# Adjacency masks of the first attention layer: comparing a quarter of the row pairs in SBUF ahead of the transpose, and copying their masks out of PSUM with ScalarE

## The chip, the cores and the metric

The kernel runs on one core of a Trainium2 chip. The metric is the device time of the whole program in microseconds (us). It was run three times; the number that counts is the median. One more execution was taken with the hardware profiler, and all views of the profile come from that one.

The engines are called by the profile's short names: PE is TensorE's matrix multiplication, PEld its weight load, DVE is VectorE, ACT is ScalarE, POOL is GpSimd, SP is SyncE, which here only issues DMAs.

## The reference

The program is two layers over a graph of 4096 nodes with 256 features each. A layer is graph attention and then a feed-forward part. What matters here is the attention of the first layer: four heads, each with 64 outputs, and an adjacency matrix of 4096 x 4096 int32 zeros and ones that masks the scores.

```python
h = jnp.einsum('nd,mdo->mno', x, W)
f_src = jnp.einsum('mno,mo->mn', h, a1)
f_dst = jnp.einsum('mno,mo->mn', h, a2)
e = jax.nn.leaky_relu(f_src[:, :, None] + f_dst[:, None, :], LEAK)
e = jnp.where(adj[None, :, :] > 0, e, NEG_INF)
attn = jax.nn.softmax(e, axis=-1)
out = jax.nn.elu(jnp.einsum('mnk,mko->mno', attn, h))
return jnp.transpose(out, (1, 0, 2)).reshape(x.shape[0], -1)
```

Node n sums over its neighbours k. On the chip k must lie on the partitions, so the kernel needs the adjacency turned: `adj[n, k]` as a mask with k on the partitions and n along the row.

## The kernel before

The function `attention` (called in line 686 for the first layer) walks over the 4096 nodes n in five column chunks of 4, 7, 7, 7 and 7 tiles of 128 nodes. For each chunk it goes over the four heads, and within a head over 16 pairs q of neighbour tiles (a tile is 128 neighbours k, so there are 32 tiles, numbered j). One chunk, head and pair is a **unit**: 64 units make a chunk, 16 a head. In a unit of a 7-tile chunk

- ScalarE makes `st`, two steps (`step_of`, line 483) of 128x896, one for each tile of the pair: whether the score is on the positive or the negative branch of the leaky relu;
- VectorE combines `st` with the mask of the pair into `m1` (line 617, 128x1792), and for two thirds of the pairs subtracts to get `m2` (line 632);
- TensorE multiplies the masks with the values (`products`, line 569), adding up in `acc`, for the unit before the present one (`LAG` is 1).

ScalarE runs two units ahead (`LEAD`, line 550). `st` and `m1` have three buffers, `m2` two. When a head is finished, ScalarE copies parts of `acc` into `lo` (line 492), VectorE adds them up into `u` (line 496), and `close` finishes the rows in small pieces during the first units of the next head; one of them is an `Exp` on ScalarE (line 521).

The masks are made only in this layer. For a pair of tiles j and j + 1, `load_rows` (line 205) lets GpSimd issue a DMA that reads 256 columns of the adjacency for the nodes of a chunk, casts them to bf16, and leaves them in `rows` (buffers of the pool `stream`, four of them). `turn` (line 214) transposes one tile's columns on TensorE into the PSUM tile `tp_m` (line 219; bf16, one buffer). `to_mask` (line 224) has VectorE compare out of PSUM into SBUF: the result is 1 or 0, or, for the pairs that `turned(q)` names (every third), 0 or -1; hence its two branches, lines 227 and 229.

This is done at two places:

- For chunk 0, `first_masks` runs in the preparation, beside the projections of the features (the first 103 us or so). The masks stay in SBUF in `m`.
- For the chunk after the present one, `make` (line 528) is a generator that the main loop takes one step further at the end of each unit (line 646). A tile is turned in one unit and compared in the next, so that nearly all of a chunk's 64 units do one half of a tile. The result goes into `ms` (two buffers of a pair each), which SP's queue writes to `edges` in DRAM (line 542); `load_mask` reads it back for the next chunk.

In the main loop VectorE and ScalarE keep the order in which the program is written, because of

```python
with tc.manual_schedule(engines={mybir.EngineType.DVE, mybir.EngineType.Activation}):
```

Everything that `make` emits in a unit is therefore placed after that unit's `step_of`, `m1`, `m2` and a piece of `close`. In the preparation the order on the engines is the framework's.

Of the kernel before, what the change touches and what calls it, by code (L numbers as in the profile page):

```python
# [16 lines left out]
OP = mybir.AluOpType  # L17
# [27 lines left out]
def gnn_ffn_kernel(ctx: ExitStack, tc: tile.TileContext, a: dict, out: bass.AP):  # L45
    nc = tc.nc
    x, adj = a["x"], a["adj"]
    N = x.shape[0]
    NT = N // P
# [75 lines left out]
    def turned(q):  # L125
        return q % 3 == 0
# [45 lines left out]
    def attention(tag, src, norm, w, others, chunks, first, ends, following):  # L172
# [7 lines left out]
        with ExitStack() as scope:  # L180
# [9 lines left out]
            masks, arow, f1b = {}, {}, {}  # L190
# [14 lines left out]
            def load_rows(c, j):  # L205
                nt = chunks[c]
                arow[c, j] = rows_in().bitcast(BF16).rearrange("p (t n) -> p t n", n=2 * P)

                nc.gpsimd.dma_start(  # L209
                    arow[c, j][:, :nt, :],  # L210
                    adj[starts[c] * P : (starts[c] + nt) * P, j * P : (j + 2) * P].rearrange("(t p) n -> p t n", p=P),
                )

            def turn(pool, c, j):

                nt = chunks[c]
                tp = pool.tile([P, 8 * P], BF16, name="tp_m")
                for t in range(nt):
                    nc.tensor.transpose(  # L219
                        tp[:, t * P : (t + 1) * P], arow[c, j - j % 2][:, t, (j % 2) * P : (j % 2 + 1) * P], ident16  # L220
                    )
                return tp

            def to_mask(dst, tp, c, j):
                w = chunks[c] * P
                if turned(j // 2):
                    nc.vector.tensor_scalar(dst[:, :w], tp[:, :w], 0.0, -1.0, op0=OP.is_le, op1=OP.add)
                else:
                    nc.vector.tensor_scalar(dst[:, :w], tp[:, :w], 0.0, None, op0=OP.is_gt)  # L229

            def first_masks(pool, j):

                g = j // 8
                if j % 8 == 0:
                    masks[0, g] = mask.tile([P, 8, CM * P], BF16, name="m")
                for jj in (j, j + 1):
                    to_mask(masks[0, g][:, jj % 8, :], turn(pool, 0, jj), 0, jj)
                if j % 8 == 6:
                    w = chunks[0] * P
                    nc.sync.dma_start(  # L240
                        edges[g * 8 : (g + 1) * 8, :, :w].rearrange("j p n -> p j n"), masks[0, g][:, :, :w]
                    )

            with ExitStack() as ps:
# [163 lines left out]
                if not first:  # L408
                    load_mask(0, 0)
                made_masks = 0  # L410
                late = [functools.partial(make, prep, small_ps, get(prep)) for get, make in others]
                for g in range(NG + 2):
                    if g + 2 < NG:
                        load(g + 2)
                    if 2 <= g < NG:
                        columns(g)
                    if 1 <= g <= NG:
                        now = products(g - 1)
                    if 2 <= g:
                        lower(g - 2)  # L420
                    if g < 2:
                        columns(g)
                    if g == 0 and late:
                        late.pop(0)()
                    if 1 <= g <= NG:
                        upper(g - 1, *now)
                    if first:
                        for _ in range(2 if g in (1, 2, 3, 4, 5, 6) else 1):
                            if made_masks < NT:
                                first_masks(ps_m, made_masks)  # L430
                                if made_masks + 6 < NT:
                                    load_rows(0, made_masks + 6)
                                made_masks += 2
                    elif g in (2, 4, 6):
                        load_mask(0, g // 2)
                    if g in (3, 5) and late:
                        late.pop(0)()
# [90 lines left out]
            def make(c):  # L528

                n0, w = starts[c] * P, chunks[c] * P  # L530
                load_rows(c, 0)
                load_rows(c, 2)
                for j in range(NT):
                    if j % 2 == 0:
                        st = made.tile([P, 2, CM * P], BF16, name="ms")
                        if j + 4 < NT:
                            load_rows(c, j + 4)
                    tp = turn(ps_m, c, j)
                    yield
                    to_mask(st[:, j % 2, :], tp, c, j)  # L540
                    if j % 2 == 1:
                        nc.sync.dma_start(
                            edges[j - 1 : j + 1, :, n0 : n0 + w].rearrange("j p n -> p j n"), st[:, :, :w]
                        )
                    if j < NT - 4:
                        yield

# [39 lines left out]
            with tc.manual_schedule(engines={mybir.EngineType.DVE, mybir.EngineType.Activation}):  # L587
# [3 lines left out]
                for at in range(len(units) + LAG):  # L591
# [5 lines left out]
                    if at < len(units):  # L597
                        c, h, q = units[at]
                        w = chunks[c] * P
                        if q == 0 and h == 0 and first and c + 1 < len(chunks):  # L600
                            making = make(c + 1)
                        if q == 4 and at + NJ < len(units):
                            load_f1(*units[at + NJ - 4][:2])
# [46 lines left out]
            c, h, q = units[-1]  # L650
# [31 lines left out]
    for n in range(2):  # L682
        av = a[f"L1_gnn_a{n + 1}"]
        for got, to in zip(weights(f"g{n + 1}", a[f"L1_gnn_W{n + 1}"], av[:, :D], av[:, D:], not n), (gw, makers)):
            to.append(got)
    attention("g0", x, True, w0, [make, *makers], [4, 7, 7, 7, 7], True, to_rows(x1d, x), [x1d])


# [272 lines left out]
    for n in range(2):  # L961
        attention(
            f"g{n + 1}",
            h1d if n else x2d,
            not n,
            gw[n],
            [],
            [8, 8, 8, 8],
            False,
            to_rows(x3d, x2d) if n else to_rows(h1d),  # L970
            [x3d, runs_of] if n else [h1d],
        )
# [7 lines left out]
    with ExitStack() as scope:  # L980
# [16 lines left out]
        with ExitStack() as rs:  # L997
# [16 lines left out]
            for g in range(NG + 2):  # L1014
# [12 lines left out]
                if 1 <= g <= NG:  # L1027
                    u = g - 1
                    t = rows.pop(u)
# [83 lines left out]
            for i in range(2):  # L1113
# [33 lines left out]
                op0=OP.mult,  # L1147
                op1=OP.is_lt,
# [206 lines left out]
        for g in range(NG + 3):  # L1355
            if g < NG:
                ys[g] = [back(g, i) for i in range(2)]
            if 3 <= g:
                for i, y in enumerate(ys.pop(g - 3)):
                    for r in range(G):  # L1360
                        t = (g - 3) * G + r
# [34 lines left out]
```

## Time and profile before

| | |
|---|---|
| median of three runs | 3407.78 us (3407.05 to 3408.95) |
| the profiled execution: time, span | 3416.7 us, 3415.0 us |
| busy share of the span | PE 92%, PEld 81%, DVE 91%, ACT 81%, POOL 37% |
| preparation of the first layer, masks of chunk 0 | about 0 to 103 us |
| chunk 0 (4 tiles), masks of chunk 1 made | about 103 to 203 us |
| chunks 1, 2, 3 (7 tiles), masks of the next chunk made | about 203 to 653 us |
| chunk 4 (7 tiles), no masks made | about 653 to 793 us |
| L227 and L229 in chunks 1 to 4 (`ms`) | 48 and 80 instructions of 618 ns |
| L227 and L229 in chunk 0 (`m`) | 12 and 20 instructions of 421 and 417 ns |
| L219, the transposes into `tp_m` | 1024 of 128x128 |

A row of the profile names line, engine, operation, the tile that is written and those that are read, and the shape. "Idle before" is the time in which the engine stood still just ahead of such instructions, and the arrow names what ended most of it. The recorded duration of an instruction can overlap with the next one's on the same engine, so the time by which an instruction holds its queue is read from the starts of two that follow each other.

### The profile page before, as it was taken

Reading aid. Unit: us, or ns where it says so; the run is one execution under the profiler, and the core shown is the slowest. Engines: PE = TensorE matmul, PEld = TensorE weight load, DVE = VectorE, ACT = ScalarE, POOL = GpSimd, SP = SyncE. Lnnn points to the kernel's source line nnn. Section 1 sums busy time; section 2 is a strip of 40 time slices with the busy share of each in tenths; the row PEclk is TensorE's granted clock in tenths of the full one; section 3 lists DMA queues with packets and bytes.
Section 4 is the critical chain, followed back from the end, with each engine's and each line's share of the span. In section 5 each row is a group of like instructions: output and inputs, shape, how many; then the busy total and the mean of one; then the engine's idle time right before and its main releaser. Section 6 shows DMA issues by size and latency. Waiting matters only on the chain.

```text
span 3415.0 us, 84150 instructions
## 1 busy us (share of the span) xinstructions
PE 3149.6 (92%) x34367; PEld 2767.7 (81%) x34367; DVE 3105.9 (91%) x5992; ACT 2754.6 (81%) x3422; POOL 1248.2 (37%) x1166
## 2 busy tenths in 40 slices
PE   7889999997999999999988999999889999985995
PEld 4788888885888888888866999999779999984884
DVE  7999999998999999999978999999899999996445
ACT  3888888897888888888857999999799999982221
POOL 3210010005999999999982000000300000002662
PEclk9999999998999999999999999999999999996997
DMA  7997886603334343334363032230503131314224
GB/s 147 174 230 145 192 184 142 193 23 86 69 68 69 69 68 67 69 69 69 67 162 119 27 119 73 75 119 24 172 20 125 33 131 50 113 48 144 89 90 186
DMA packets 533659, 351.63 MB, mean 103 GB/s; under 512 B 350589, under 2 KB 483866, under 8 KB 533274
## 3 DMA queue, kind: packets, MB, share of 16 engines
q1 hardware_dynamic: 452210, 287.12, 30.8%
q0 software_dynamic: 73920, 52.97, 9.9%
q10 hardware_dynamic: 7144, 6.16, 0.6%
q8 instruction: 271, 4.44, 0.5%
q14 instruction: 114, 0.93, 0.1%
HBM read 248.01 MB, written 68.81 MB: 93 GB/s over the span
## 4 chain that ended last, share of the span: by engine, by line
DVE 32%; POOL 31%; issue 15%; PE 14%; ACT 6%; DMA 2%; ACTq 0%; DVEq 0%; POOLq 0%; SPq 0%
DVE m L617 17%; POOL th L869 16%; PE acc L569 10%; POOL z_rs L892 7%; ACT st L483 4%; POOL z_rs L893 3%; DVE rows L632 3%; DVE m L632 2%; POOL yd L1316 2%; POOL gx L1250 2%; DVE u L496 1%; DVE v L382 1%; DVE ms L229 1%; PE ph L308 1%; DVE u L506 1%
## 5 line engine op out<-in xcount | busy, mean ns | idle before, releaser
L569 PE MATMUL acc<-vals,m 128*128 128x130 f16 (+1 forms) x19456 | 1722.1, 233 | 72.3 <-DVE m L632 42.8
L483 ACT ACTIVATE st<-f1b,f2b 128x1024 bf16<-128x1024 f32 (+2 forms) x1664 | 1659.1, 1073 | 98.9 <-DVE m L617 92.4
L569 PEld LDWEIGHTS <-m 128*128 128x128 bf16 x19456 | 1516.9, 98 | 170.6 <-DVE m L632 65.0
L617 DVE TENSOR_TENSOR m<-st,m 128x2048 bf16<-128x2048 bf16 (+2 forms) x832 | 929.1, 1134 | 15.2 <-ACT st L483 14.9
L569 PE MATMUL acc<-vals,rows 128*128 128x130 f16 x5120 | 614.1, 221 | 15.1 <-DVE rows L632 15.1
L905 PE MATMUL po<-wT,zT 128*128 128x256 f32 x1920 | 575.6, 382 | 7.0 <-ACT zT L888 7.0
L908 PE MATMUL po<-w,zT 128*128 128x256 f16 x3840 | 577.4, 273 | 1.9 <-DMA zT<-z 1.9
L869 POOL TENSOR_TENSOR th<-th,y 128x1024 f32<-128x1024 f32 x240 | 569.2, 2372 | 25.4 <-ACT th L868 5.6
L908 PEld LDWEIGHTS <-zT 128*128 128x128 f16 x3840 | 376.1, 98 | 163.0 <-DMA zT<-z 2.9
L569 PEld LDWEIGHTS <-rows 128*128 128x128 bf16 x5120 | 490.0, 96 | 20.5 <-DVE rows L632 20.1
L632 DVE TENSOR_TENSOR rows<-m,m 128x2048 bf16<-128x2048 bf16 x320 | 391.7, 1224 | 10.2
L845 DVE SCALAR_TENSOR_TENSOR y<-po,z_rs,bias 128x256 f32<-128x256 f32 x928 | 384.4, 477 | 1.9 <-PE tp L838 0.7
L881 DVE BATCH_NORM_STATS2 z_st<-z 128x6 f32<-128x256 f32 x960 | 335.8, 413 | 0.0
L905 PEld LDWEIGHTS po<-wT,zT 128*128 128x128 f32 x1920 | 290.7, 191 | 16.9 <-ACT zT L888 8.6
L106 POOL TENSOR_TENSOR ln_rstd<-ln_rstd,mhalf 128x4 f32<-128x4 f32 x24 | 34.1, 1421 | 645.4 <-DVE ln_rstd L105 630.5
L857 ACT ACTIVATE z<-th 128x1024 f32<-128x1024 f32 x240 | 251.2, 1047 | 8.6 <-POOL th L869 8.3
L209 POOL DMA_DIRECT2D rows<-in_adj_dram x80 | 72.8, 910 | 492.9 <-PE tp_m L219 479.8
L868 ACT ACTIVATE th<-y 128x1024 f32<-128x1024 f32 x240 | 249.8, 1041 | 0.0
L892 POOL TENSOR_TENSOR z_rs<-z_rs,mhalf 128x4 f32<-128x4 f32 x240 | 245.8, 1024 | 0.0
L888 ACT COPY zT<-tp 128x512 f32<-128x512 f32 x240 | 140.4, 585 | 109.0 <-PE tp L838 108.9
L632 DVE TENSOR_TENSOR m<-m,m 128x1792 bf16<-128x1792 bf16 (+1 forms) x200 | 202.2, 1011 | 13.1 <-PE acc L569 0.5
L462 POOL MEMSET hs<- 128x4 f32 x3 | 0.3, 101 | 582.3 <-DVE u L513 582.3
(251 smaller groups left out, 3165.1 us busy)
## 6 DMA issues: line engine op xcount, KB each, us to landing
m<-edges SPq DMA_DIRECT2D x32, 2048.0 KB
rows<-in_adj_dram POOLq DMA_DIRECT2D x64, 448.0 KB
edges<-ms SPq DMA_DIRECT2D x64, 448.0 KB
m<-edges SPq DMA_DIRECT2D x16, 1792.0 KB
f1b<-fd SPq DMA_DIRECT2D x32, 512.0 KB
rows<-x1d SPq DMA_DIRECT2D x16, 512.0 KB
y<-yd SPq DMA_DIRECT2D x16, 512.0 KB
f1b<-fd SPq DMA_DIRECT2D x16, 448.0 KB
```

The lines of the kernel that those rows point to most:

```text
L483: nc.scalar.activation(steps[at][:, s, :w], f1b[c, h][:, :w], AF.Relu, bias=f2b[:, 2 * q + s, h : h + 1], scale=BIG)
L569: nc.tensor.matmul(acc[:, i, cols], lhs[:, s, rows], v[:, cols], start=(j == 0 and n_ == 0), stop=(j == NT - 1 and n_ == 1), skip_group_ch ...
L617: nc.vector.tensor_tensor(m1[:, :, :w], st[:, :, :w], m, OP.logical_and if turned(q) else OP.min)
L632: nc.vector.tensor_tensor(m2[:, :, :w], m, m1[:, :, :w], OP.subtract)
L845: nc.vector.scalar_tensor_tensor(y[:, g * G + r, :], po[:, r, :], rstd[:, r : r + 1], last if end else bias, op0=OP.mult, op1=OP.add,)
L857: nc.scalar.activation(z, th.pop(u), AF.Silu, scale=0.01)
L868: nc.scalar.activation(th[at], y[:, g * G : (g + 1) * G, :], AF.Tanh, scale=0.01)
L869: ins = nc.gpsimd.tensor_tensor(th[at], th[at], y[:, g * G : (g + 1) * G, :], OP.add)
L881: nc.vector.bn_stats(st[:, r, :], z[:, r, :])
L892: nc.gpsimd.tensor_tensor(rs[u], rs[u], mhalf, OP.pow)
L905: nc.tensor.matmul(po[:, r, :], src[:, r * P : (r + 1) * P], wT, start=True, stop=False)
L908: nc.tensor.matmul(po[:, r, :], src16[:, part * G + r, :], w16[:, other, :], start=False, stop=(part == 1 and other == 1),)
```

## The change

The function `compared` picks the tile pairs 1, 5, 9 and 13 of the 16: a quarter. For these pairs `compare` runs on VectorE over the loaded rows in SBUF, in place, both tiles of the pair and all tiles of the chunk in one instruction (128x1792 bf16, in chunk 0 128x1024), before TensorE turns them. The comparison is the same as that of `to_mask`, with 1 and 0 or 0 and -1. TensorE then transposes finished masks, and `to_mask` has ScalarE copy them from PSUM, two copies for a pair (128x896, in chunk 0 128x512). The other twelve pairs of a chunk are left as they were.

In `make` the comparison for the pair that begins at j + 1 is placed just after the second tile of the pair before has been turned into a mask and its write to `edges` was issued; in `first_masks` it stands ahead of the pair's transposes. The loads of the rows, the number of transposes, the buffers and the writes to `edges` stay.

```diff
+            def compared(j):
+
+                return j // 2 % 4 == 1
+
+            def compare(c, j):
+
+                t = arow[c, j][:, : chunks[c], :]
+                if turned(j // 2):
+                    nc.vector.tensor_scalar(t, t, 0.0, -1.0, op0=OP.is_le, op1=OP.add)
+                else:
+                    nc.vector.tensor_scalar(t, t, 0.0, None, op0=OP.is_gt)
+
             def to_mask(dst, tp, c, j):
                 w = chunks[c] * P
-                if turned(j // 2):
+                if compared(j):
+                    nc.scalar.copy(dst[:, :w], tp[:, :w])
+                elif turned(j // 2):
                     nc.vector.tensor_scalar(dst[:, :w], tp[:, :w], 0.0, -1.0, op0=OP.is_le, op1=OP.add)
                 else:
                     nc.vector.tensor_scalar(dst[:, :w], tp[:, :w], 0.0, None, op0=OP.is_gt)
...
                 g = j // 8
+                if compared(j):
+                    compare(0, j)
                 if j % 8 == 0:
...
                             edges[j - 1 : j + 1, :, n0 : n0 + w].rearrange("j p n -> p j n"), st[:, :, :w]
                         )
+                        if j + 1 < NT and compared(j + 1):
+                            compare(c, j + 1)
                     if j < NT - 4:
                         yield
```

## The prediction

> **What bounds the kernel now.** The change touches only the first attention layer, so I read the engines' busy time by stretch first. The three stretches below lie in column chunks 1, 2 and 3, each of which also makes the masks of the chunk after it. Columns: stretch, its length, then busy us and instruction counts of PE, PEld, DVE, ACT, POOL, the TensorE clock, the DMA share, GB/s.
>
> ```profile
> 205.00:350.00 145.00, 134.62 (x1927) 124.53 (x1927) 137.22 (x169) 124.53 (x137) 14.88 (x16) 0.99 0.80 180
> 355.00:500.00 145.00, 135.20 (x1946) 124.68 (x1945) 138.49 (x169) 124.21 (x136) 14.87 (x16) 1.00 0.76 168
> 505.00:650.00 145.00, 134.85 (x1942) 124.37 (x1940) 138.14 (x168) 123.86 (x136) 11.16 (x12) 1.00 0.74 170
> ```
>
> VectorE is busy 95%, TensorE 93%, ScalarE 86%. No engine has much room, so shares don't decide. The waits do (who waited, for whom: total, times, longest; 105 to 650 us):
>
> ```profile
> ACT st L483 <- DVE m L617: 72.4, 113, 2.4
> PEld L569 <- DVE m L632: 52.0, 96, 1.4
> PE acc L569 <- DVE m L632: 34.6, 90, 1.3
> DVE u L496 <- ACT lo L492: 13.9, 27, 1.0
> ```
>
> ScalarE and TensorE both wait for VectorE's masked pairs; VectorE waits for them only at the change of head (`u` after `lo`). The chain of waits over 0 to 700 us tells where in a head (start, length, piece):
>
> ```profile
> 420.49 1.73 PE acc L569 x27
> 422.61 3.96 PE acc L569 x56
> 426.96 3.00 PE acc L569 x44
> 432.42 1.08 DVE m L632
> ...
> 457.90 1.73 PE acc L569 x27
> ```
>
> The same pieces come back after 457.90 − 420.49 = 37.4 us: one head (16 units), 2.34 us a unit. For 9.5 us before a head ends the chain is TensorE's; from 432 to 458 it is VectorE's. So VectorE work in those 26 us lengthens the head, as long as TensorE can follow. That is where the changed pair falls.
>
> **What the mask work costs.** From the instructions on tile `tp_m`:
>
> ```profile
> L229 DVE TENSOR_SCALAR ms<-tp_m x80: 615/618/620, 112.4 to 643.4; 128x896 bf16<-128x896 bf16 x80
> L229 DVE TENSOR_SCALAR m<-tp_m x20: 402/417/426, 30.0 to 99.8; 128x512 bf16<-128x512 bf16 x20
> ```
>
> Recorded 0.618 us, but the queue is held less. The timeline has one comparison and its successor:
>
> ```profile
> 448.04 0.62 DVE L227 TENSOR_SCALAR ms<-tp_m 128x896 bf16<-128x896 bf16 x1
> 448.31 5.69 ACT L483 ACTIVATE st<-f1b,f2b 128x896 bf16<-128x896 f32 x6
> 448.57 1.08 DVE L617 TENSOR_TENSOR m<-st,m 128x1792 bf16<-128x1792 bf16 x1
> ...
> 455.70 1.79 PE L569 MATMUL acc<-vals,m 128*128 128x130 f16 x28 [0.33 <-DVE m L632]
> ...
> 457.90 1.73 PE L569 MATMUL acc<-vals,m 128*128 128x130 f16 x27 [0.41 <-DVE m L632]
> ```
>
> 448.57 − 448.04 = 0.53 us per comparison: successive VectorE instructions overlap by about 0.08. The six ScalarE steps take 5.69 / 6 = 0.95 each. The bracketed waits are TensorE's room, used below.
>
> **What the Trainium skill says.** Page "VectorE: DVE Perf Modes", section "The perf-mode tier table": `tensor_scalar` on bf16 runs at four elements a cycle from SBUF, at most two from PSUM. The trace agrees on the second (896 elements at two a cycle of 0.96 GHz are 467 ns, plus some 150, against 618); it has no bf16 SBUF `tensor_scalar`, so the four are not shown. Page "SBUF — State Buffer", section "SBUF: two separate sides": a VectorE op in a two-port mode and a GpSimd op exclude each other for a whole instruction, descriptor writing for GpSimd's DMAs included. No run here shows that; its cover is below.
>
> **The change, part by part.** In chunks 1 to 4 a head of 16 units turns 8 mask rows, four pairs; one pair changes, always the head's second. 4 × 4 = 16 pairs, plus 4 in chunk 0.
>
> *Removed:* two PSUM comparisons per pair on VectorE, 2 × 0.535 = 1.07 us (chunk 0: 2 × 0.34 = 0.68, from 0.418 less the 0.08).
>
> *Added on VectorE:* one in-place comparison of 128x1792. The page's walk-through ("Side-by-side", about 158 cycles fixed) gives, as an estimate, (1792/4 + 158) / 0.96 = 0.63 us, held 0.55. Bounds: 0.47 if only the elements counted; 1.00 at two a cycle, as the 128x1792 `tensor_tensor` row L617 holds the queue; 1.9 at one. I take 0.55. Chunk 0, 128x1024: 0.43, held 0.35. **VectorE saves 1.07 − 0.55 = 0.52 per pair, 0.33 in chunk 0.** All: 16 × 0.52 + 4 × 0.33 = 9.6 us.
>
> *Added on ScalarE:* two copies per pair. No 128x896 PSUM copy exists, but two sizes of `scalar.copy` out of PSUM do:
>
> ```profile
> L328 ACT COPY hc<-ph 128x512 f32<-128x512 f32 x48 | 26.4, 582 | 20.6 <-DVE fs L322 18.9 <-DVE fs L326 1.6
> L279 ACT COPY xT<-tp 128x1024 f32<-128x1024 f32 x16 | 16.2, 1012 | 26.3 <-PE tp L114 26.2
> ```
>
> 582 + (384/512) × 430 = 905 ns, held 0.82 (lower if bf16 out were cheaper, upper 0.95 as the steps of L483): 1.64 us per pair. Its cover is ScalarE's idle time, 145 − 124.2 = 20.8 us in 3.9 heads, **5.4 per head**.
>
> *Where they stand in the queues.* Counting units from the head's start, `compare` follows the comparison in unit 3, the copies end units 5 and 7.
> - VectorE: 0.55 later from unit 3, level after unit 5, 0.52 ahead after unit 7. TensorE's turn of that pair comes in unit 4, after `products(3)`, at 440.07 in this head; the comparison would end near 439.3, so TensorE doesn't wait for it.
> - ScalarE: the first copy follows the step for unit 7, which ends near 441.8; the turn it reads ends at 440.6. No wait. The next step started at 442.69 (after a wait for VectorE): the 0.82 fits. The second copy follows the step for unit 9 and the head's `Exp`, near 448.3. It pushes the six steps at 448.31 back by 0.82, to end at 454.8. The step for unit 12 is then done near 454.8 and is used at 458.3; the waits at 454.55, 456.68 and 459.41 swallow the delay.
> - TensorE: the turn at 449.95 needs `tp_m` back (one buffer); the second copy ends at 449.2. It then catches up by its waits of 0.28, 0.33 and 0.41 after 450: 1.0 against 0.52 needed. So nearly all of the 0.52 gets through; I count 0.50.
> - DMA queues: each row load is awaited by a turn about 30 us after it is issued (20 in chunk 0's stage), and a 448 KB load takes a few us, so VectorE's new wait for it ends at once. GpSimd's load issues (0.93 us) run right after the second turn of a pair, over a us before `compare`; they waited 447 us anyhow. SP's write of the pair waits for the second copy rather than for VectorE, about 0.6 us later; nothing but loads for the next head is behind it.
>
> *Sum.* Chunks 1 to 3: 12 heads × 0.50 = 6.0. Chunk 0's stage (103 to 203 us, 24.9 us a head, the 16 DMA engines busy all through): the ScalarE waits that follow the copies, 0.47 and 0.59 in the head at 128 us, are less than twice 0.82, so ScalarE hands on only some 0.3 of the 0.52: 4 × 0.3 = 1.2. Masks of chunk 0 in the preparation: VectorE is busy 78 of 105 us there, with much waiting for others, so 0.8 of 1.3. **Together 8.0 us** of the profiled execution's 3416.7 (span 3415.0). That execution was 8.9 above the median 3407.78; the stage is 1/6 of it, so I take 8.0 off the median: **3399.8 us**. What is late next is TensorE: after the 0.5 its room at the end of a head is 0.5 more.
>
> **Rivals.**
> 1. *Gain swallowed* (TensorE ends last): it is the chain for 9.5 us of every head, and its spare time is only some 2.6 us of 37.4. If it can't follow by more than a third, or the comparison runs at two elements a cycle (saving 0.07), 0 to 4 us remain: 3404 to 3408. Against: the three waits above sum to 1.0.
> 2. *ScalarE becomes the bound, slower.* It has run some 2.5 us ahead of VectorE at the copies (441.8 against 444.3). If it must sit there until VectorE's old time, for the turn or for the buffer `ms` to be written out, each copy costs 0.82 + 2.5, a head 6.6 against 5.4 of room. From 5.4 − 1.64 = 3.8 us of such waiting per head it decides: here +1.2 a head and no saving, 12 heads +14, and chunk 0's stage about +2: 3424. For: `ms` was waited for twice by VectorE (2.6 us), in chunk 0's stage and just after. Against: the 13 us between the write's issue and the copy in chunks 1 to 3.
> 3. *The change doesn't do what it says* (comparison at one element a cycle, held 1.9): per pair +0.8, 16 pairs +13, less where hidden: about 3417.
>
> **Numbers.** Forecast 0.64, rival 1 0.20, rivals 2 and 3 together 0.16. A measurement of this kernel tells about 0.2%, 6.8 us, from no change. The forecast's own range is 3397.5 to 3403 and lies across that border (3401.0): I give 0.48 of its 0.64 to faster by over 0.2%; rival 1 and the rest of it make 0.37 within; slower 0.15 of the last 0.16. Range 3396 to 3410: below, all 9.6 us and 2 more for a comparison near its lower bound; above, rival 1 and the first us of rival 2.
>
> **What would show it.** In the profile after: 16 rows of an in-place `rows` comparison near 0.63 us (at 1.08 or 2.0 rival 1 or 3); 32 ScalarE copies near 0.9; L617's wait by ScalarE falling from 72 to about 50 us; the head in chunks 1 to 3 at 36.9 instead of 37.4. I am wrong if VectorE waits for `st` inside a head, if the copies show long waits for TensorE or DMA, or if the head is 37.4 with TensorE's waits near nothing.

## The result, and the profile after

The changed kernel takes 3412.41 us (median of 20 runs, 3409.03 to 3416.82), the kernel before 3408.32 us in the same comparison. The ratio is 1.0014, with a 95% interval of 1.0008 to 1.0020: 4 us slower, where 8 us faster was forecast.

The spans of the two profiled executions say the opposite, 3407.5 us after and 3415.0 before, and mislead: the last head of the first layer's attention has its first `lo` row at 792.3 us before and at 793.6 after. Behind it lie only parts that the change doesn't touch, and there before took 2622.7 us and after 2613.9, 8.8 less; in the four profiled executions of the first group of experiments it was 2613.3 to 2614.5. So before's profile was long at its end, and only the first 793 us are compared here.

Most of the forecast can still be found in them. Busy time by stretch, in the three stretches that the prediction showed (stretch, length, busy us and counts of PE, PEld, DVE, ACT, POOL, clock, DMA share, GB/s):

```profile
205.00:350.00 145.00, 132.88 (x1936) 124.10 (x1935) 136.25 (x166) 131.93 (x146) 13.95 (x15) 1.00 0.76 168
355.00:500.00 145.00, 133.66 (x1949) 124.56 (x1947) 136.83 (x164) 130.13 (x144) 13.95 (x15) 1.00 0.77 169
505.00:650.00 145.00, 134.86 (x1967) 125.63 (x1965) 137.93 (x166) 131.00 (x145) 11.16 (x12) 1.00 0.72 168
```

ScalarE has taken on 5.9 to 7.4 us a stretch; VectorE does less and is still the busiest. The new operations, from the instructions on `tp_m` and on `rows` (count, min/median/max ns). Five more in-place comparisons, of the pairs with 0 and -1, are in line 232, and the eight copies of chunk 0's masks have a row of their own:

```profile
L239 ACT COPY ms<-tp_m x32: 880/882/886, 110.4 to 637.8; 128x896 bf16<-128x896 bf16 x32
```
```profile
L234 DVE TENSOR_SCALAR rows<-rows x15: 407/615/618, 21.5 to 628.2; 128x1792 bf16<-128x1792 bf16 x12, 128x1024 bf16<-128x1024 bf16 x3
```

The waits over 105 to 650 us (an extract) have a line in them that was small before, VectorE's for `edges` (2.6 us in two waits, the longest 1.8):

```profile
ACT st L499 <- DVE m L635: 53.3, 82, 9.5
...
PE tp_m L219 <- DVE ms L241: 12.7, 4, 8.6
DVE ms L241 <- DMA edges<-ms: 11.6, 3, 9.0
```

VectorE stands still for 9.0 us until a write of `ms` to `edges` has landed, and the other engines with it: ScalarE waits up to 9.5 for `m`, TensorE 8.6 for `ms`. The chain of waits over 100 to 850 us has three such writes on it (start, length):

```profile
187.60 14.31 DMA edges<-ms
338.82 9.84 DMA edges<-ms
488.58 9.87 DMA edges<-ms
```

All three lie in the last head of a chunk, chunks 0, 1 and 2. The same list for before has only one (189.54, 8.10). How long each head takes is read from the start of its first `lo` row on ScalarE; a head counts here from one such row to the next, us. "Chunk 0, last" and "chunk 1, first" are neighbours and share what is early or late between them.

| kernel | chunk 0, heads 2 and 3 | chunk 0, last | chunk 1, first | chunks 1 to 3, others | last of chunks 1, 2 |
|---|---|---|---|---|---|
| before | 24.91, 24.90 | 29.02 | 36.64 | 37.40 | 37.86, 37.87 |
| changed | 24.44, 24.44 | 36.09 | 35.24 | 36.94 | 38.95, 38.97 |

An ordinary head is 0.46 us shorter. The last heads give it all back and more: +7.1, +1.1 and +1.1, of which the head after chunk 0's returns 1.4. From the first of these rows to the last it is 665.2 us before and 668.1 after, 2.9 longer.

SP's queue shows why the write is late there. In the last head of a chunk, SP issues not only the writes of `ms` but also the loads of the next chunk's masks, 1792 KB each. First before, then changed (start and length of the issue; "x2" are two in a row):

```profile
183.57 0.36 SPq L201 DMA_DIRECT2D m<-edges  x1
189.54 0.36 SPq L542 DMA_DIRECT2D edges<-ms  x1
189.99 0.42 SPq L201 DMA_DIRECT2D m<-edges  x1
```
```profile
181.10 5.97 SPq L201 DMA_DIRECT2D m<-edges  x2
187.60 0.36 SPq L558 DMA_DIRECT2D edges<-ms  x1
```

Before, load, write, load. In the changed kernel load, load, write: the write of the copied pair (pair 13, the last head's second) has gone behind the second mask load. `manual_schedule` names VectorE and ScalarE only, so SP's order is the framework's. What made it place this write later is not shown; that it waits for ScalarE's second copy instead of VectorE is the likely reason, for the old order is back in a run below that leaves pair 13 alone. The write is 448 KB; issued just behind 1792 KB it landed 14.3 us later, against 8.1 before. VectorE needs that buffer, one of two, for the first comparison of pair 15:

```profile
191.08 0.62 DVE L243 TENSOR_SCALAR ms<-tp_m 128x896 bf16<-128x896 bf16 x1
...
201.99 0.62 DVE L241 TENSOR_SCALAR ms<-tp_m 128x896 bf16<-128x896 bf16 x1 [8.97 <-DMA edges<-ms]
```

The place is also the tightest one. `make` leaves out its second `yield` for the last four tiles, so pair 15 follows pair 13 after four units, where other pairs have six. From the issue of a write to the moment when the engine that fills its buffer next, two pairs on, is ready to do so, the changed kernel has 11.6 to 14.0 us in chunks 1 to 3, but 8.6, 8.6 and 8.5 after pair 13; in chunk 0's stage it is 6.5 to 9.7 and 5.4. A landing of 14.31 us against 5.4 makes the wait of 8.97; 9.84 and 9.87 against 8.6 make two of 1.3. In chunk 3 the order is exchanged too (loads at 629.85 and 638.05, write at 638.74), but VectorE doesn't wait for the buffer there, so the write landed within 8.5 us, and that head is 37.56.

This was a reading of one trace. The experiments test it.

### The profile page after: what moved, and what is told of

The parts are those of the page before. It is cut to its first block, busy times and chain, and to the rows that moved or that the text cites. A ratio compares the mean times of both kernels' runs of the same rounds, so it can differ in the third digit from the quotient of the medians.

```text
span 3407.5 us, 84203 instructions
## 1 busy us (share of the span) xinstructions
PE 3142.2 (92%) x34367; PEld 2768.6 (81%) x34367; DVE 3098.5 (91%) x5972; ACT 2779.7 (82%) x3462; POOL 1243.8 (37%) x1166
## 4 chain that ended last, share of the span: by engine, by line
PE 35%; DVE 30%; issue 14%; POOL 9%; ACT 8%; DMA 3%; DVEq 0%; POOLq 0%; SPq 0%; ACTq 0%
DVE m L635 17%; PE po L926 10%; PE po L923 10%; PE acc L587 9%; ACT st L499 5%; DVE rows L650 3%; PE tp L856 3%; POOL th L887 2%; POOL yd L1334 2%; POOL gx L1268 2%; DVE m L650 2%; POOL z_rs L910 1%; DVE u L512 1%; DMA edges<-ms 1%; DVE u L522 1%
```

## The experiments

Three theories stood at the start. **A**: the exchanged order on SP's queue costs it, through VectorE's wait for the buffer. **B**: a faster VectorE and the copies crowd the last head, whatever the order. **C**: ScalarE's copies take what VectorE gains. Each group of runs had its own runs of the kernel before beside it (3408.2 us in the first group, 3418.0 and 3419.4 in the other two), so ratios are compared.

### SP's order written by hand, in both kernels

```diff
-with tc.manual_schedule(engines={mybir.EngineType.DVE, mybir.EngineType.Activation}):
+with tc.manual_schedule(
+    engines={mybir.EngineType.DVE, mybir.EngineType.Activation, mybir.EngineType.SP}
+):
```

Expected of the changed kernel with this edit:

> The changed kernel with SP's queue added to the engines that keep the written order in the main loop, so that the write of the copied pair stands ahead of the second mask load in the last head of a chunk. Theory A (SP's order: in the changed kernel the planner put that mask load ahead of the write, and VectorE then waited for its buffer): the long wait for 'edges' near 193 us goes, the last heads shrink to 37.4 or less (chunk 0: from 36.1 to under 29), and the time falls by 8 to 11 us against the changed kernel, to about 3401; ratio to before 0.998. Theory B (the copies and the faster VectorE bunch writes and loads in the last head, whatever the order): the wait stays, 3408 to 3413. Theory C (ScalarE's copies cost what VectorE gains): no head gets shorter, 3411.

And of the kernel before with it:

> The kernel before with SP's queue kept in the written order in the main loop: the control for the first run. A, B and C: within 2 us of before (3408), since there the write stood ahead of the load already; what it differs by is the price of the written order of the other SP transfers.

Measured: the changed kernel 3403.80 us, ratio 0.9986 (0.9979 to 0.9992); the kernel before 3408.87 us, ratio 1.0004 (0.9996 to 1.0012). The write of pair 13 stands ahead of the load again, it is issued at 187.01, and the wait at 194.98 is 2.55 us instead of 8.97:

```profile
187.01 0.36 SPq L558 DMA_DIRECT2D edges<-ms  x1
187.47 0.41 SPq L201 DMA_DIRECT2D m<-edges  x1
...
194.98 0.62 DVE L241 TENSOR_SCALAR ms<-tp_m 128x896 bf16<-128x896 bf16 x1 [2.55 <-DMA edges<-ms]
```

Chunk 0's last head and the one after it take 66.1 us together, against 65.7 before and 71.3 in the changed kernel; the last heads of chunks 1 and 2 are 37.55. The control doesn't move, so writing the order by hand is by itself worth nothing to the kernel before; with the change it is worth about 9 us. That is A. The time is 3 us above the 3401 that A named, and the last heads are a little over its figures too (29.3 in chunk 0 for "under 29", 37.55 for "37.4 or less").

### Only the pairs of the first three heads

```diff
-                return j // 2 % 4 == 1
+                return j // 2 in (1, 5, 9)
```

> The changed kernel with compared() true for the pairs 1, 5 and 9 only, so that the last head of each chunk, in which the mask loads of the next chunk are issued, is as before, and SP's order there too. A: the heads 1 to 3 keep their 0.47 us (12 x 0.47 = 5.6) and the preparation about 1.2: 3401 to 3402, ratio 0.998. B: the same if the copies of the last head are what does the harm; if a faster VectorE does it, the wait stays and it is 3405 to 3411. C: 3410.

Measured: 3402.04 us, ratio 0.9983 (0.9974 to 0.9992). Heads 1 to 3 keep 36.94; chunk 0's last head and its neighbour take 66.2 us together, and SP issues load, write, load there again (180.72, 186.68, 187.14). A faster VectorE in three heads out of four doesn't bring the wait back, so B holds at most for what happens in the last head itself. C fails in this run and the one above: the ordinary heads keep what they gained.

### The kernel before with the two transfers exchanged

This run has no comparison in SBUF and no copy. It is the second run above with the write of pair 13 issued one unit later, so that it falls behind the mask load:

```diff
                     if j % 2 == 1:
+                        if j // 2 == 13:
+                            yield
                         nc.sync.dma_start(
                             edges[j - 1 : j + 1, :, n0 : n0 + w].rearrange("j p n -> p j n"), st[:, :, :w]
                         )
-                    if j < NT - 4:
+                    if j < NT - 4 and j // 2 != 13 or j == 26:
                         yield
```

> The kernel before with SP's queue in the written order, as in the second run, and one thing changed: the write of pair 13 is issued after the second mask load of the last head instead of ahead of it. No comparison in SBUF and no copy by ScalarE. A: VectorE waits near 193 us for 'edges', chunk 0's last head grows from 29 to about 36 us and those of chunks 1 and 2 by about 1 us each: 8 to 10 us slower than the second run, about 3417. B and C: no more than 2 us slower than the second run.

Measured: 3424.00 us, ratio 1.0041 (1.0028 to 1.0055), 15 us over its control. The last heads of chunks 0, 1 and 2 are 39.2, 41.0 and 42.0 us against 30.0, 37.9 and 37.9 in the control: 9.2, 3.1 and 4.1, some 16 in all. SP and VectorE's waits (105 to 660 us and the queue):

```profile
184.55 5.70 SPq L201 DMA_DIRECT2D m<-edges  x2
190.35 1.55 SPq L544 DMA_DIRECT2D edges<-ms  x1
```
```profile
DVE ms L227 <- DMA edges<-ms: 16.4, 3, 11.6
```

Exchanging two transfers is enough to make the loss, without anything of the change. It is more than the 3417 that A named and more than in the changed kernel. The write was not issued late: 0.12 us after its second comparison ended (189.61 + 0.62). But in the chain of waits it took 17.84 us to land (14.31 in the changed kernel), and 11.14 and 12.11 in chunks 1 and 2 (9.84 and 9.87). Why it took longer is open.

### Three buffers for `ms`, order left as it was

```diff
-                made = scope.enter_context(tc.tile_pool(name=f"{tag}_made", bufs=2))
+                made = scope.enter_context(tc.tile_pool(name=f"{tag}_made", bufs=3))
```

> The changed kernel, SP's order left swapped, with three buffers for ms instead of two. Theory A1 (what costs is VectorE's wait for a free ms buffer behind the late write): the 9 us wait for 'edges' goes, chunk 0's last head falls from 36 to about 29 us, time about 3402 (8 to 10 under the changed kernel). Theory A2 (the late order itself costs: the mask loads hold SP's queue and the DMA engines, so that masks of the next chunk arrive late, whatever VectorE does): the last head stays above 34, or the first head of chunk 1 grows by as much; 3408 or more.

> The kernel before with three buffers for ms: the control. A1: its two short waits (2.6 us in all) go, chunk 0's last head falls from 29 to some 27: 3405 to 3408. A2: as before, 3408.

Measured: the changed kernel 0.9975 (0.9967 to 0.9983), 8.9 us under before; the kernel before 0.9990 (0.9984 to 0.9997), 2.8 us under. In the changed kernel the write still stands behind the second load,

```profile
187.75 0.36 SPq L201 DMA_DIRECT2D m<-edges  x1
188.64 0.36 SPq L558 DMA_DIRECT2D edges<-ms  x1
```

but no line of VectorE's waits names `edges`, and chunk 0's last head and its neighbour are down to 61.9 us (62.8 in the control). So what the exchange costs is VectorE's wait for a buffer; the masks aren't late because of it. Between the two kernels with three buffers, 0.9975 / 0.9990 = 0.9985: the change is worth about 5 us once the buffer is not what ends the wait.

### The preparation alone

`compared` true for chunk 0 only:

> The change for chunk 0's masks alone (compared() only in the preparation); the main loop's masks as before. If VectorE bounds the preparation: 1 to 2.5 us faster than before (3406 to 3407). If the shorter preparation of the changed kernel's profile (102.2 against 104.4 us) is scatter or an effect of the order: 3408 plus or minus 1.

Measured: ratio 0.9999 (0.9991 to 1.0008). In the profiles the preparation is shorter with the change (`hs`, its last step on ScalarE, starts at 100.6 to 103.3 us in the nine profiles whose preparation has it, 102.9 here, and at 104.4 to 106.2 in the four without), but the time doesn't show it. Whether a gain of under 3 us is there stays open.

### Which pair of a head, and how many

The first try took two pairs of each of the first three heads:

```diff
-                return j // 2 % 4 == 1
+                return j // 2 in (1, 3, 5, 7, 9, 11)
```

> Half of the pairs of the first three heads compared in SBUF (pairs 1, 3, 5, 7, 9 and 11), none in the last head, where SP's order is as before. VectorE is relieved of twice 0.47 us a head. If VectorE remains the bound and the others follow: heads of 36.4 to 36.5 instead of 37.4, 12 x 0.95 = 11 and the preparation 2 to 3: about 3395. If TensorE ends last, or ScalarE with two more copies (room of 3.6 us a head against 1.8 more): heads stay at 36.7 to 37, 3399 to 3402.

Measured: ratio 1.0046 (1.0033 to 1.0060), heads of 38.55 us. Neither of my cases came: the worse of them still had heads of 36.7 to 37, and these are over a microsecond longer than before. The wait of `u` for `lo` had risen from 12.6 to 28.4 us (205 to 650 us), which pointed to the place of the second copy, not to the number. Three runs for that: the second and third pair (`j // 2 % 4 in (1, 2)`, three buffers), the last pair alone (`j // 2 in (3, 7, 11)`), and the third alone (`j // 2 % 4 == 2`, three buffers):

> Three buffers for ms, and two pairs of every head compared in SBUF, the second and the third (copies by ScalarE in units 5, 7, 9 and 11), so that no copy stands in the last units of a head. Theory P (the place counts: in the run with pairs 1 and 3 the copies in units 13 and 15 put ScalarE late for the change of head): heads of 36.4 to 36.7, ratio to before 0.995 to 0.997. Theory Q (two pairs are too many for ScalarE wherever they stand): heads of 37.5 to 38.5 as in that run, ratio 1.000 to 1.004.

> Only the last pair of each of the first three heads of a chunk (3, 7 and 11) compared in SBUF; copies in units 13 and 15; two buffers for ms, SP's order as before. P: the heads grow to 37.6 to 38.6 although VectorE has 0.5 less to do, ratio 1.001 to 1.004. Q: one pair is one pair, heads of 36.9, ratio 0.998.

> Three buffers for ms, and the third pair of every head (copies in units 9 and 11) in place of the second. P: heads of 36.9, as with the second pair, SP's order not swapped: ratio 0.997 to 0.998. If already units 9 and 11 are late for the change of head: heads of 37.2 or more, ratio 0.999 or above. Q: 36.9.

| pairs of a head | ratio to before (95%) | ordinary head, us |
|---|---|---|
| none (before) | 1 | 37.40 |
| second, three buffers | 0.9975 (0.9967 to 0.9983) | 36.94 |
| third, three buffers | 0.9992 (0.9983 to 1.0000) | 37.44 |
| second and third, three buffers | 1.0006 (0.9998 to 1.0014) | 37.50 |
| last, heads 1 to 3 | 1.0053 (1.0039 to 1.0066) | 39.01 |
| second and last, heads 1 to 3 | 1.0046 (1.0033 to 1.0060) | 38.55 |

One pair in the last place costs 1.6 us a head though VectorE has less to do; the second pair added to it takes 0.46 off again, as it does alone. With one pair in a head, then, the place decides, which is P. But the third alone gave what its expectation named as the case against, 37.44, and the second and third together gave the figures of Q (two pairs are too many wherever they stand), not P's 36.4 to 36.7.

The chains of waits tell the cases apart. Before, the part of a head that VectorE ends has five comparisons on the chain (for one head at 396.10, 400.85, 406.99, 410.72 and 415.50); the other three fall in the last 9.5 us, which TensorE ends. With the second pair there are three and the in-place one (389.23, 393.98, 408.16; 394.51), one row fewer. With the third pair it is four and the in-place one:

```profile
430.76 0.53 DVE ms L243
...
435.51 0.53 DVE ms L243
...
441.65 0.53 DVE ms L241
...
445.38 0.54 DVE ms L241
445.92 0.53 DVE rows L234
```

Only one of the third pair's two comparisons stood in VectorE's part, and the in-place one took its place: nothing is saved, and no copy of ScalarE's is on this chain. With the second and third pair together the chain of the last 21 us of a head (from 449.36 in one of them) is ScalarE's alone, steps and copies in a row: there four copies are too many. The change of head in the run with the last pair alone, ScalarE's timeline:

```profile
432.39 3.84 ACT L499 ACTIVATE st<-f1b,f2b 128x896 bf16<-128x896 f32 x4
436.14 0.88 ACT L239 COPY ms<-tp_m 128x896 bf16<-128x896 bf16 x1
436.93 1.97 ACT L499 ACTIVATE st<-f1b,f2b 128x896 bf16<-128x896 f32 x2
438.81 0.58 ACT L508 ACTIVATE lo<-acc 128x520 f32<-128x520 f32 x1
```
```profile
438.07 0.55 PE L219 MATMUL tp_m<-ident,rows 128*128 128x128 bf16 x7
440.17 4.12 PE L587 MATMUL acc<-vals,m 128*128 128x260 f16 x56 [1.55 <-DVE u L512]
```
```profile
439.42 0.70 DVE L512 TENSOR_TENSOR u<-acc,lo 128x520 f32<-128x520 f32 x1 [2.06 <-ACT lo L508]
```

ScalarE works without a gap from the copy of unit 13, at 431.61, to `lo`. TensorE is through with the head's products by 438.2; `lo` starts at 438.81, because steps and copies of the coming units stand ahead of it on ScalarE; `u` waits 2.06 for it, and TensorE, which needs `acc` emptied, 1.55. Over 205 to 650 us the wait of `u` for `lo` is 28.7 us in this run, 22.1 with the second and third pair and 12.4 with the second alone.

## Why the prediction was wrong

**VectorE bounds the heads, and the saving gets through: right.** 0.50 a head was forecast for chunks 1 to 3; 37.40 became 36.94, 0.46. In chunk 0's stage 0.47 got through where I counted 0.3: ScalarE didn't hold it back. The third pair's run agrees with the reading behind it, that VectorE's work counts only ahead of TensorE's last 9.5 us.

**The prices: right.** The comparison took 0.615 us for an estimated 0.63 (0.407 to 0.420 for 0.43 in chunk 0), so the four elements a cycle that the Trainium skill's page "VectorE: DVE Perf Modes" states in "The perf-mode tier table" are there. The copy took 0.882 for 0.905. ScalarE's wait for `m` fell from 72.4 to 53.3, for "about 50".

**ScalarE hides the copies: right for this pair.** The 5.4 us a head are a sum, though, and the other runs show that it can't be spent anywhere: two copies of 0.88 in the last units cost 1.6 us a head, and four copies a head leave ScalarE the last to end.

**The failed step is the one on the DMA queues**: "SP's write of the pair waits for the second copy rather than for VectorE, about 0.6 us later; nothing but loads for the next head is behind it." The time was right: in the heads of chunks 1 to 3 the write is issued 0.53 us later. So is the rest in three heads out of four. In the last head of a chunk the neighbour is a mask load four times the size of the write, and SP's order isn't written by hand. I took the order of the queue as given and moved only the time, and put its cost at nothing. What the runs showed in its place: the load goes ahead of the write, the write lands 14.3 us after its issue, and VectorE waits for the buffer. The price of that: +7.1, +1.1 and +1.1 in the last heads, and up to 8.97 us in one wait. With the order restored the kernel is 4.4 us under before; with a third buffer 8.9, of which the buffer alone gives the kernel before 2.8. So 4 to 6 us of the 8.0 are there; the preparation's 0.8 and part of the last heads' share (0.30 a head for 0.50, with the third buffer) were not found.

**The sum for chunk 0's stage** gave −1.2; in the profiles the stage, from `hs` to the first `lo` row of chunk 0's last head, went from 101.5 to 108.3 us, +6.8. The prediction says in that place that the 16 DMA engines are busy all through, and draws nothing from it. **The preparation**, 0.8, could not be shown in the time.

**The rivals.** None was it. Rival 2 named the buffer `ms` as a wait and chunk 0's stage as its place, which was near, but it put the wait on ScalarE, let it begin beyond 3.8 us a head in all heads, and argued against it with "the 13 us between the write's issue and the copy". That margin is there for the other pairs of chunks 1 to 3, but after pair 13 it is 8.6, and 5.4 in chunk 0's stage. The argument would have needed the tightest place, and the question which transfer is ahead of which there.

## What to carry to other kernels

When an instruction gets a new releaser, ask on every queue whose order is left to the framework what may now be placed ahead of it, and look at the stretch where the largest transfers are issued, not at the average one. When a DMA empties a double buffer, compare its landing with the time until the buffer is needed at the tightest place: here 14.3 us against 5.4. One more buffer of `ms` took the changed kernel from 1.0014 to 0.9975 of before, about 13 us, more than the 8 that the change was forecast to give. And idle time of an in-order engine is not a sum to be spent anywhere: what stands just ahead of the copy-out that ends an accumulation can be on the path, even on an engine that is idle 14% of the time; here it cost 1.6 us a head. Nor is a saving worth the same everywhere: the third pair's comparisons were taken off VectorE and the head stayed at 37.44.

## What the runs showed of the hardware

- A 448 KB write issued right behind a 1792 KB load landed after 14.3 us in chunk 0's stage, after 9.8 and 9.9 in chunks 1 and 2, and within 8.5 in chunk 3. Issued right ahead of the load in chunk 0's stage it took 7.9 to 8.7 (before, and the two runs with SP's order by hand). The DMA share over the landings of 14.3, 9.8 and 9.9 was 1.19, 1.06 and 1.15 (packets count by their start, so it can pass 1); over the 10 us after the write in chunk 3 it was 0.94.
- The in-place bf16 comparison of 128x1792 in SBUF takes as long as the 128x896 one out of PSUM (0.615 and 0.617 us). The Trainium skill's page "SBUF — State Buffer" says in "SBUF: two separate sides" that VectorE's two-port modes and GpSimd exclude each other. No run here shows it, and they hardly test it: in the main loop GpSimd's load issues (0.93 us) start 1.2 us or more ahead of the comparisons, and only one of the 20 comparisons, in the preparation, overlaps an issue.
- Of the versions run, the fastest against before is the changed kernel with three `ms` buffers, ratio 0.9975 (0.9967 to 0.9983).
